# Last q and k of a batch kept on chip, v1, scores and the loads of x moved in a fused attention and triangle kernel

## The chip, the cores and the metric

One core of one Trainium2 chip. The metric is the device time of one execution in microseconds (us), lower is better. Most executions of a kernel agree within 0.3%. A ratio is the mean time of one kernel's runs over that of the kernel before in the same rounds on the same chip, so it is not quite the ratio of the medians that I quote. "Within 2%" counts as the same.

## The reference, cut to what matters

Input x has 4 batches of 64 x 64 tokens of 256 channels, all in float32. Layer 0 is self-attention over the 4096 tokens, layer 1 is a "triangle" attention followed by a layer norm, an MLP and a second layer norm.

```python
# layer 0
f, g, v = xt @ Wf + bf, xt @ Wg + bg, xt @ Wh + bh
beta = softmax(einsum('bqd,bkd->bqk', g, f))
x1 = x + (einsum('bqk,bkd->bqd', beta, v) @ Wo + bo)
# layer 1: 8 heads of 32
q, k, v1, v2 = (x1 @ W for W in (Wq, Wk, Wv1, Wv2))
scores = einsum('bilhd,bljhd->biljh', q, k) / sqrt(d_k)
att = softmax(scores, axis=2)
out = einsum('biljh,bilhd,bljhd->bijhd', att, v1, v2)
h = layer_norm(x1 + out @ Wo1)
out = layer_norm(relu(h @ W1 + b1) @ W2 + b2 + h)
```

## The kernel before

Each batch runs through three stages. In the **attention stage** TensorE computes layer 0, and between its products it projects the finished blocks of 512 tokens to q, k, v1 and v2, which go to DRAM. The **transition** finishes the last block, and computes the first scores of the triangle. The **triangle stage** has 4 pairs of heads with 8 steps each, 32 steps. In a step VectorE (DVE) and GpSimd (POOL) form eight products att x v2, TensorE sums them with v1 in its stationary tile ("wsel") into PSUM accumulators ("acc"), and ScalarE (ACT) copies these out. In every odd step the next pair's scores ("sp") are made as well. From batch 1 on, the MLP of the batch before fills holes of the step.

The profile lines leave numbers out of names. In them gf is g and f of one block of x, ahg and ahf are their places in DRAM, tp and yT are the turned block in PSUM and on chip, R and Rp are the products that DVE and POOL form, v1c is the loaded v1, S the scores after the exponential, es the weights, ao the copy of acc; nt, hT, mp, hid and zp belong to the MLP and its layer norms.

At the start, x of batch 0 comes block by block, each load issued just before it is turned. The tags name the buffer rings; "R" has three buffers, "qk" one:

```python
def turned(q):                                   # front0
    if q % 2 == 0:
        xt[q // 2] = work.tile([P, 8, C], F32, tag="R", name="xt", bufs=3)
    t = xt[q // 2][:, q % 2 * 4 : q % 2 * 4 + 4, :]
    nc.sync.dma_start(out=t, in_=xf[b, ts(q, 512), :]...)
    ...                                          # 8 transposes
for q in range(8):
    ahead = turned(q + 1) if q < 7 else None
    factors(...)                                 # g and f
    for w, n in enumerate(("g", "f")):
        nc.scalar.dma_start(out=d[n][q], in_=gf[:, w, 0:P])
    if ahead: taken(*ahead)                      # ScalarE and DVE copy the turned block
    ...                                          # v
    if q % 4 == 3: ...                           # spreads of g and f, sync queue
```

The end of the transition, where the last q and k pass through DRAM:

```python
proj(last, "q", 0, None, stage[0][:, 2, :])
proj(last, "k", 0, None, stage[0][:, 3, :])
L.fetch_qk(0, 1)                                 # the part just stored
...
more = [v1, q, k, v2 of the last block, second halves]
for u in range(4):
    L.scores(0, u); L.take_scores(); more[u]()
```

The start of a step:

```python
if step == 1: L.fetch_qk(1)
if scored: L.scores(pair + 1, ig // 2)
if waiting is not None:
    L.take(step - 1, 1, waiting); L.store(step - 1)
if step == 2: L.fetch_v2(1)
if ig == 0 and 0 < pair < NPAIR - 1: L.fetch_v2(pair + 1)
L.fetch_v1(step + 2)
if scored: L.take_scores() ...
if more and not late: L.stationary(step + 1)
L.product(step, Q_[0]); L.product(step, D_[0])
...
```

Of the kernel before, what the change touches and what calls it, by code (L numbers as in the profile page):

```python
# [33 lines left out]
def attention_then_triangle_kernel(  # L34
# [164 lines left out]



    def spread_g(F, r, d, q0=0, q1=8):
        nc.sync.dma_start(
            out=F.gT[ts(r, CQK), 512 * q0 : 512 * q1].rearrange("c (q t) -> c q t", t=P),
            in_=d[q0:q1].rearrange("q (n c) t -> c (q n) t", n=4),
        )

    def spread_f(F, q, d):
        nc.sync.dma_start(
            out=F.fT[ts(q % 4, CQK), q // 4, :].rearrange("c (n t) -> c n t", t=P),  # L210
            in_=d[q].rearrange("(n c) t -> c n t", n=4),
        )


    def front0(b):
        F = Front()
        for name in ("x0", "x1", "g", "f", "lo", "hi"):
            F.alloc(name)
        d = {n: dram.tile([8, P, P], F32, tag="ah" + n, name="ah" + n, bufs=NB) for n in ("g", "f")}
        xt = {}  # L220

        def turned(q):
            if q % 2 == 0:
                xt[q // 2] = work.tile([P, 8, C], F32, tag="R", name="xt", bufs=3)
            t = xt[q // 2][:, q % 2 * 4 : q % 2 * 4 + 4, :]
            nc.sync.dma_start(out=t, in_=xf[b, ts(q, 512), :].rearrange("(n p) c -> p n c", p=P))
            tp = pa("tp")
            for cc in range(2):
                for n in range(4):
                    nc.tensor.transpose(tp[:, cc, ts(n, P)], t[:, n, ts(cc, P)], ident)  # L230
            return q, tp

        def taken(q, tp):
            nc.scalar.copy(F.yT[0][:, ts(q, 512)], tp[:, 0, :])
            nc.vector.tensor_copy(F.yT[1][:, ts(q, 512)], tp[:, 1, :])

        taken(*turned(0))
        for q in range(8):
            ahead = turned(q + 1) if q < 7 else None
            col = ts(q, 512)  # L240
            gf = work.tile([P, 2, C], F32, tag="s4", name="gf")
            factors(pb("gf"), [F.yT[cc][:, col] for cc in range(2)], gf)
            for w, n in enumerate(("g", "f")):
                nc.scalar.dma_start(out=d[n][q], in_=gf[:, w, 0:P])
            if ahead:
                taken(*ahead)
            ps = pc("vp")
            for n in range(4):
                for cc in range(2):
                    nc.tensor.matmul(  # L250
                        ps[:, ts(n, P)], F.yT[cc][:, ts(q * 4 + n, P)], wh_sb[:, cc, :],
                        start=(cc == 0), stop=(cc == 1),
                    )
            nc.vector.tensor_copy(
                F.v[q // 4][:, q % 4 * 4 : q % 4 * 4 + 4, :], ps.rearrange("p (n d) -> p n d", n=4)
            )
            if q % 4 == 3:
                for r in range(4):
                    spread_f(F, q - 3 + r, d["f"])
                    spread_g(F, r, d["g"], q - 3, q + 1)  # L260
        return F


# [80 lines left out]
    def layer0(b, F, safe, rest):  # L344
# [152 lines left out]
        def proj1(qb, m, ps=None, st=None, queue=nc.sync):  # L497
# [11 lines left out]
                in_=st.rearrange("p (n c) -> p n c", n=2),  # L509
            )  # L510

        parts = [
            [norm, bounds],
            [output],
# [9 lines left out]
        for g in range(8 * NQB):  # L524
            qb, k = divmod(g, 8)
            if safe and k == 0 and qb + 1 < NQB:
                mx, todo = pieces(qb + 1)
                for qc, t in todo:
                    max_piece(qc, t, mx)
                row[qb + 1] = max_row(mx)  # L530
            if g + 1 < 8 * NQB:
                scores(g + 1)
            values(g)

            if qb > 0 and not (qb == last and k >= 6):
                for part in parts[k]:
                    part(qb - 1)
            if qb == last and k == 3:
                L.fetch_v1(0)
                L.fetch_v1(1)  # L540
            if qb == last and k == 5:
                if b > 0:
                    rest.load(NP * (b - 1))
                L.fetch_qk(0, 0)
        L.fetch_v2(0, 0)


# [14 lines left out]
        bounds(last)  # L562
        if old:
            rest.affine_a(t0)
            rest.turn(t0)
        proj(last, "q", 0, None, stage[0][:, 2, :])
        proj(last, "k", 0, None, stage[0][:, 3, :])
        L.fetch_qk(0, 1)
        if old:
            rest.load(t0 + 1)  # L570
            rest.residue(t0)
            mps = [rest.hidden(t0, fc, wide=True) for fc in range(4)]
            for fc in range(4):
                rest.rectify(t0, fc, mps[fc])
# [9 lines left out]
        for u in range(4):  # L584
            L.scores(0, u)
            L.take_scores()
            more[u]()
        L.sums(0)
        L.weights(0)
        L.turn(0)  # L590
# [7 lines left out]
    class Layer1:  # L598
# [6 lines left out]



        def fetch_qk(self, pair, part=None):
            io, rows = self.io, ts(pair, 64)
            if part != 1:  # L610
                self.qk[pair] = big.tile([P, 2, 2048], F32, tag="qk", name="qk")
            qk = self.qk[pair]
            i0, i1 = ((0, 56), (56, 64))[part] if part is not None else (0, 64)
            for lh in range(2):
                half = slice(64 * lh, 64 * lh + 64)
                nc.sync.dma_start(
                    out=qk[half, 0, 32 * i0 : 32 * i1],
                    in_=io["q"][rows, lh, i0:i1, :].rearrange("c i l -> c (i l)"),
                )
                a, e = max(i0 - 32 * lh, 0) * N, min(i1 - 32 * lh, 32) * N  # L620
                if a < e:
                    nc.sync.dma_start(
                        out=qk[half, 1, a:e], in_=io["k"][rows, 2048 * lh + a : 2048 * lh + e]
                    )


        def fetch_v2(self, pair, part=None):
# [336 lines left out]
    def run_layer1(b, L, rest, ahead, F):  # L964
# [7 lines left out]
        for step in range(NSTEP):  # L972
# [12 lines left out]
            k = L.npool(step)  # L985
            D_, Q_ = list(range(8 - k)), list(range(8 - k, 8))
            scored = step % 2 == 1 and pair + 1 < NPAIR
            if step == 1:
                L.fetch_qk(1)
            if scored:  # L990
                L.scores(pair + 1, ig // 2)
            if waiting is not None:
                L.take(step - 1, 1, waiting)
                L.store(step - 1)
# [1 line left out]
                L.fetch_v2(1)  # L996
            if ig == 0 and 0 < pair < NPAIR - 1:
                L.fetch_v2(pair + 1)
            L.fetch_v1(step + 2)
            if scored:  # L1000
                L.take_scores()
                if ig == 7 and pair + 2 < NPAIR:
                    L.fetch_qk(pair + 2)
            if more and not (scored and ig == NIG - 1):
                L.stationary(step + 1)

            late = scored and ig == NIG - 1

# [11 lines left out]
            L.accumulate(step, D_[0])  # L1020
            if behind is not None:
                ahead.values(behind)
            if more and late:
                L.stationary(step + 1)
            if not late:
                next_weights()
            if odd_a:
                rest.affine_a(nxt)
            if odd:
# [43 lines left out]
            if odd_a:  # L1073
                rest.rectify(nxt, 0, mps[0])
                rest.rectify(nxt, 1, mps[1])
            L.accumulate(step, Q_[1])
            if odd_a:
                mps = [rest.hidden(nxt, 2), rest.hidden(nxt, 3)]
                rest.rectify(nxt, 2, mps[0])
# [86 lines left out]
```

## Time and profile before

| | before |
|---|---|
| median of the first 3 runs | 4058.42 us (4054.1 to 4064.45) |
| profiled span, mean granted clock | 4059.6 us, 0.983 |
| TensorE (PE) busy | 93% |
| start, to the first scores of batch 0 | 54.65 us |
| first scores to the first attP copy, batch 0 | 458.95 us |
| steps of pairs 0 to 2, batch 0 | 361.3 us |
| the same, batches 1 to 3 together | 1181.7 us |

"attP copy" is ScalarE's copy of turned attention weights. It happens once a step, so 128 of these copies mark all steps; "pairs 0 to 2" runs from the first copy of a batch to the copy 25 steps later. From the page, the clock row (tenths in 40 slices of the span) and the last chain:

```profile
PEclk8999989999999999999999999999999998999999
...
PE 70%; DMA 7%; DVE 7%; ACT 6%; POOL 4%; issue 4%; SPq 2%; ACTq 0%; POOLq 0%; DVEq 0%
PE o L419 23%; PE acc L754 12%; PE proj L476 8%; PE s L397 7%; PE mp L893 5%; DVE R L745 4%; PE zp L908 4%; DMA v1c<-v1d 4%; POOL Rp L745 3%; PE v1p L501 3%; PE hp L800 2%; PE sp L650 2%; ACT es L687 2%; DMA qk<-k 1%; PE y L461 1%
```

The clock dips below 0.9 in the start, in the triangle stage of batch 0 and once late in batch 3. Loads of v1 (4%) and of q and k (1%) stand on the chain that ended last. The waits of batch 0's triangle stage (columns: total us, times, longest) name the same two:

```profile
ACT wsel L723 <- DMA v1c<-v1d: 13.7, 3, 6.5
...
PE sp L650 <- DMA qk<-k: 10.6, 2, 6.3
```

### The profile page before, as it was taken

How to read it: one execution, taken by the hardware profiler on the slowest of the kernel's cores; microseconds unless marked ns; L12 is line 12 of the kernel's file. 1: busy time of each engine (PE TensorE's matmuls, PEld its weight loads, DVE VectorE, ACT ScalarE, POOL GpSimd, SP SyncE). 2: the span in 40 equal slices, each digit the busy share in tenths (PEclk: the TensorE clock that was granted, in tenths of full speed). 3: DMA queues.
4: the chain of work that ended last, by engine and by line, in shares of the span. 5: the costliest groups of instructions: out<-in, count | busy, mean ns of one | idle time of the engine just before them, and what ended most of it. 6: DMA issues, size and time to landing. Idle time of an engine off the chain costs nothing.

```text
span 4059.6 us, 58989 instructions
## 1 busy us (share of the span) xinstructions
PE 3768.2 (93%) x23238; PEld 1761.1 (43%) x23238; DVE 2696.2 (66%) x2183; ACT 1812.7 (45%) x3737; POOL 1899.5 (47%) x976
## 2 busy tenths in 40 slices
PE   8999978889999989998999989999899998999988
PEld 4444433433444444443344444444344444444466
DVE  3444378897444379899544458899744437998955
ACT  2333355554333355554333345555433334555444
POOL 1000078895000079999000048899500007999944
PEclk8999989999999999999999999999999998999999
DMA  4111444543111433323111153232211143331122
GB/s 111 50 50 47 107 121 131 142 125 121 47 47 50 110 85 83 84 49 85 59 50 47 52 124 87 62 82 63 85 47 47 50 109 85 82 83 43 46 63 59
DMA packets 445199, 311.45 MB, mean 77 GB/s; under 512 B 298672, under 2 KB 410288, under 8 KB 437616
## 3 DMA queue, kind: packets, MB, share of 16 engines
q1 hardware_dynamic: 428320, 297.15, 27.6%
q10 hardware_dynamic: 15280, 7.54, 0.7%
q8 instruction: 185, 3.03, 0.3%
q0 software_dynamic: 1312, 2.89, 0.3%
q14 instruction: 102, 0.84, 0.1%
HBM read 166.93 MB, written 140.51 MB: 76 GB/s over the span
## 4 chain that ended last, share of the span: by engine, by line
PE 70%; DMA 7%; DVE 7%; ACT 6%; POOL 4%; issue 4%; SPq 2%; ACTq 0%; POOLq 0%; DVEq 0%
PE o L419 23%; PE acc L754 12%; PE proj L476 8%; PE s L397 7%; PE mp L893 5%; DVE R L745 4%; PE zp L908 4%; DMA v1c<-v1d 4%; POOL Rp L745 3%; PE v1p L501 3%; PE hp L800 2%; PE sp L650 2%; ACT es L687 2%; DMA qk<-k 1%; PE y L461 1%
## 5 line engine op out<-in xcount | busy, mean ns | idle before, releaser
L745 POOL TENSOR_TENSOR Rp<-attP,v 128x2048 f32<-128x2048 f32 x328 | 1490.4, 4569 | 713.0 <-ACT attP L704 586.6
L745 DVE TENSOR_TENSOR R<-att,v 128x2048 f32<-128x2048 f32 x696 | 1549.7, 2274 | 141.1 <-PE acc L754 90.1
L426 DVE TENSOR_TENSOR esum<-esum,e 128x2048 f32<-128x2048 f32 x224 | 512.8, 2289 | 592.3 <-ACT e L408 589.4
L754 PE MATMUL acc<-R,wsel 128*32 128x512 f32 x5568 | 730.3, 607 | 41.6 <-DVE R L745 38.3
L408 ACT ACTIVATE e<-s 128x1024 f32<-128x1024 f32 x512 | 496.6, 1021 | 408.3 <-PE s L397 380.6
L839 POOL TENSOR_SCALAR nt<-mv 128x4 f32<-128x4 f32 (+1 forms) x51 | 9.8, 193 | 1276.8 <-DVE mv L817 1272.7
L762 ACT COPY ao<-acc 128x1024 f32<-128x1024 f32 x256 | 259.2, 1012 | 597.6 <-PE acc L754 524.0
L419 PE MATMUL o<-e,vlo 128*128 128x512 f32 x1024 | 477.7, 610 | 0.0
L419 PE MATMUL o<-e,vhi 128*128 128x512 f32 x1024 | 472.7, 605 | 0.0
L754 PE MATMUL acc<-Rp,wsel 128*32 128x512 f32 x2624 | 340.9, 602 | 89.5 <-POOL Rp L745 44.0
L419 PEld LDWEIGHTS o<-e,vlo 128*128 128x128 f32 x1024 | 185.8, 191 | 283.7 <-issue 282.2
L397 PE MATMUL s<-gT,fT 32*128 32x512 f32 x2048 | 303.3, 641 | 4.8 <-ACT e L408 4.5
L419 PEld LDWEIGHTS o<-e,vhi 128*128 128x128 f32 x1024 | 184.7, 190 | 279.3 <-issue 279.3
L754 PEld LDWEIGHTS acc<-R,wsel 128*32 128x32 f32 x5568 | 143.8, 110 | 333.0 <-issue 200.9
L893 PE MATMUL mp<-hT,w 128*128 128x256 f32 x1024 | 253.2, 394 | 30.1 <-ACT hT L873 30.1
L687 ACT ACTIVATE es<-S,rd 128x64 f32<-128x64 f32 x1024 | 258.5, 335 | 8.7 <-DVE rd L679 7.1
L438 DVE RECIPROCAL rec<-den 128x512 f32<-128x512 f32 x32 | 107.4, 3358 | 215.6 <-PE den L436 215.6
L908 PE MATMUL zp<-w,hid 128*128 128x256 f32 x1024 | 246.1, 386 | 0.6 <-ACT hid L900 0.6
L893 PEld LDWEIGHTS mp<-hT,w 128*128 128x128 f32 x1024 | 185.8, 192 | 108.1 <-ACT hT L873 48.3
L908 PEld LDWEIGHTS zp<-w,hid 128*128 128x128 f32 x1024 | 187.1, 191 | 62.0 <-issue 40.2
L754 PEld LDWEIGHTS acc<-Rp,wsel 128*32 128x32 f32 x2624 | 70.2, 109 | 286.6 <-POOL Rp L745 108.1
L488 ACT COPY st<-proj 128x512 f32<-128x512 f32 x104 | 60.9, 585 | 293.7 <-issue 166.5
(140 smaller groups left out, 3791.9 us busy)
## 6 DMA issues: line engine op xcount, KB each, us to landing
v<-v2d SPq DMA_DIRECT2D x24, 1024.0 KB
v1c<-v1d SPq DMA_DIRECT2D x128, 128.0 KB
aT<-ao SPq DMA_DIRECT2D x1024, 16.0 KB
A<-aT SPq DMA_DIRECT2D x256, 64.0 KB
yc<-y SPq DMA_DIRECT2D x64, 256.0 KB
out_dram<-z SPq DMA_DIRECT2D x64, 256.0 KB
y<-yT SPq DMA_DIRECT2D x56, 256.0 KB
q<-st SPq DMA_DIRECT2D x56, 256.0 KB
```

Source lines behind the costliest of these rows:

```text
L397: nc.tensor.matmul(s_ps[r // 2][:, r % 2, :], fT[rows, tt, ts(n, P)], gT[rows, ts(qb, QB)], start=True, stop=not safe,)
L408: nc.scalar.activation(e[g][:, 2 * j : 2 * j + 2, :], s_ps[j], AF.Exp)
L419: nc.tensor.matmul(o_ps[qb], F.v[tt][:, r * 4 + n, :], es[:, r, :], start=(k == 0 and r == 0), stop=(k == 7 and r == 3),)
L426: nc.vector.tensor_tensor(esum[qb], esum[qb], es, ALU.add)
L476: nc.tensor.matmul(ps, w[:, cc, rows], y(qb, cc), start=(cc == 0), stop=(cc == 1))
L501: nc.tensor.matmul(ps[:, ts(n, C)], y(qb, cc)[:, ts(m * 2 + n, P)], wv1_sb[:, cc, :], start=(cc == 0), stop=(cc == 1),)
L687: nc.scalar.mul(self.e[:, i, :], rows[:, i, :], rec[:, i : i + 1])
L745: eng.tensor_tensor(R, src.unsqueeze(1).to_broadcast([P, D, N]), v2[:, h], ALU.mult)
L754: nc.tensor.matmul(acc[32 * c : 32 * c + 32, n % 2, :], w[:, n, c, 16 * h : 16 * h + 32], R[:, ts(c, 8), :].rearrange("p d j -> p (d j)"), ...
L762: nc.scalar.copy(self.ao[step][:, ts(np, 2)].rearrange("p k d j -> p k (d j)"), acc)
L893: nc.tensor.matmul(self.mp[:, fc % 2, :], w1_sb[:, cc, ts(fc, P)], self.hT[tt][:, cc, :], start=(cc == 0), stop=(cc == 1),)
L908: nc.tensor.matmul(self.zp[tt][:, n, :], self.hid[tt][:, fc, ts(n, P)], w2_sb[:, fc, :], start=(fc == 0), stop=(fc == 3),)
```

## The change

It has four parts: (1) all eight loads of x go first in the sync queue, the spreads of g and f move to GpSimd, and a block's g and f get a ring of three buffers of their own; (2) the last q and k of a batch are projected on two column halves so that ScalarE can copy them straight into the triangle's tile; (3) q and k of pair 1 are asked for at the end of the transition, and v1 at the start of a step, ahead of v2 and of the stores; (4) the scores move from the start of the odd step to the end of the even one, and the stationary tile is copied after the weights. The core of the diff:

```diff
+        for q in range(8):
+            nc.sync.dma_start(out=xt[q], in_=xf[b, ts(q, 512), :]...)
 ...
-                    spread_g(F, r, d["g"], q - 3, q + 1)
+                    spread_g(F, r, d["g"], q - 3, q + 1, nc.gpsimd)
 ...
+            two_halves(ps[0][:, 0:256], wq_sb, (one, one), halves)
+            two_halves(ps[1], wk_sb, (two, one), (ys, ys))
+            nc.scalar.mul(qk[:, 0, 1792:2048], ps[0][:, 0:256], scale1)
+            nc.scalar.copy(qk[64:128, 1, 1536:2048], ps[1][64:128, :])
 ...                                    (rows of pair 1: stage, three stores on ScalarE)
-        proj(last, "q", 0, None, stage[0][:, 2, :])
-        proj(last, "k", 0, None, stage[0][:, 3, :])
-        L.fetch_qk(0, 1)
+        proj_qk(L.qk[0], stage[0][:, 2:4, :])
 ...
             more[u]()
+        L.fetch_qk(1)
 ...
-            if step == 1:
-                L.fetch_qk(1)
+            L.fetch_v1(step + 2)
             if scored:
-                L.scores(pair + 1, ig // 2)
+                L.take_scores()
 ...
             L.accumulate(step, Q_[1])
+            if step % 2 == 0 and pair + 1 < NPAIR:
+                L.scores(pair + 1, ig // 2)
```

More of the change, by code (lines that the diff above doesn't have):

```diff
@@ L198, in factors, with spread_g @@
             nc.scalar.activation(t[:, w, 0:P], ps[:, w, :], AF.Identity, bias=bias)
-    def spread_g(F, r, d, q0=0, q1=8):
-        nc.sync.dma_start(
+    def spread_g(F, r, d, q0=0, q1=8, queue=nc.sync):
+        queue.dma_start(
             out=F.gT[ts(r, CQK), 512 * q0 : 512 * q1].rearrange("c (q t) -> c q t", t=P),
@@ L206, in spread_g, with spread_f @@
         )
-    def spread_f(F, q, d):
-        nc.sync.dma_start(
+    def spread_f(F, q, d, queue=nc.sync):
+        queue.dma_start(
             out=F.fT[ts(q % 4, CQK), q // 4, :].rearrange("c (n t) -> c n t", t=P),
@@ L219, in front0 @@
         d = {n: dram.tile([8, P, P], F32, tag="ah" + n, name="ah" + n, bufs=NB) for n in ("g", "f")}
-        xt = {}
-        def turned(q):
-            if q % 2 == 0:
-                xt[q // 2] = work.tile([P, 8, C], F32, tag="R", name="xt", bufs=3)
-            t = xt[q // 2][:, q % 2 * 4 : q % 2 * 4 + 4, :]
-            nc.sync.dma_start(out=t, in_=xf[b, ts(q, 512), :].rearrange("(n p) c -> p n c", p=P))
-            tp = pa("tp")
+        xt = [work.tile([P, 8, C], F32, tag="R", name="xt", bufs=3) for _ in range(3)]
+        xt.append(work.tile([P, 8, C], F32, tag="Rp", name="xt"))
+        xt = [xt[q // 2][:, q % 2 * 4 : q % 2 * 4 + 4, :] for q in range(8)]
+        for q in range(8):
+            nc.sync.dma_start(out=xt[q], in_=xf[b, ts(q, 512), :].rearrange("(n p) c -> p n c", p=P))
+        def turned(q):
+            t, tp = xt[q], pa("tp")
             for cc in range(2):
@@ L240, in front0 @@
             col = ts(q, 512)
-            gf = work.tile([P, 2, C], F32, tag="s4", name="gf")
+            gf = work.tile([P, 2, C], F32, tag="st", name="gf", bufs=3)
             factors(pb("gf"), [F.yT[cc][:, col] for cc in range(2)], gf)
@@ L258, in front0 @@
                 for r in range(4):
-                    spread_f(F, q - 3 + r, d["f"])
-                    spread_g(F, r, d["g"], q - 3, q + 1)
+                    spread_f(F, q - 3 + r, d["f"], nc.gpsimd)
+                    spread_g(F, r, d["g"], q - 3, q + 1, nc.gpsimd)
         return F
@@ L510, in proj1, with proj_qk, two_halves @@
             )
+        def proj_qk(qk, st):
+            ys = [y(last, cc) for cc in range(2)]
+            halves = [[t.rearrange("p (i o l) -> p o i l", o=2, l=32)[:, lh] for t in ys] for lh in range(2)]
+            ps = [pb("projq"), pb("projk"), pb("projq")]
+            def two_halves(ps, w, cols, moving):
+                for cc in range(2):
+                    for lh in range(2):
+                        nc.tensor.matmul(
+                            ps[ts(lh, 64), :], w[:, cc, cols[lh]], moving[lh][cc], start=(cc == 0), stop=(cc == 1)
+                        )
+            one, two = slice(0, 64), slice(64, 128)
+            two_halves(ps[0][:, 0:256], wq_sb, (one, one), halves)
+            two_halves(ps[1], wk_sb, (two, one), (ys, ys))
+            nc.scalar.mul(qk[:, 0, 1792:2048], ps[0][:, 0:256], scale1)
+            nc.scalar.copy(qk[64:128, 1, 1536:2048], ps[1][64:128, :])
+            two_halves(ps[2][:, 0:256], wq_sb, (two, two), halves)
+            nc.scalar.copy(st[0:64, 0, :], ps[1][0:64, :])
+            nc.scalar.dma_start(out=io["k"][64:128, ts(last, QB)], in_=st[0:64, 0, :])
+            nc.scalar.mul(st[:, 1, 0:256], ps[2][:, 0:256], scale1)
+            for lh in range(2):
+                nc.scalar.dma_start(
+                    out=io["q"][64:128, lh, ts(last, 8), :].rearrange("c i l -> c (i l)"),
+                    in_=st[ts(lh, 64), 1, 0:256],
+                )
         parts = [
@@ L543, in layer0 @@
                     rest.load(NP * (b - 1))
-                L.fetch_qk(0, 0)
+                L.fetch_qk(0, True)
         L.fetch_v2(0, 0)
@@ L564, in layer0 @@
             rest.affine_a(t0)
+        proj_qk(L.qk[0], stage[0][:, 2:4, :])
+        if old:
             rest.turn(t0)
-        proj(last, "q", 0, None, stage[0][:, 2, :])
-        proj(last, "k", 0, None, stage[0][:, 3, :])
-        L.fetch_qk(0, 1)
-        if old:
             rest.load(t0 + 1)
@@ L604, in __init__, with fetch_qk @@
             self.S, self.v2, self.qk, self.v1, self.att, self.ao = {}, {}, {}, {}, {}, {}
-        def fetch_qk(self, pair, part=None):
+        def fetch_qk(self, pair, first=False):
             io, rows = self.io, ts(pair, 64)
-            if part != 1:
-                self.qk[pair] = big.tile([P, 2, 2048], F32, tag="qk", name="qk")
-            qk = self.qk[pair]
-            i0, i1 = ((0, 56), (56, 64))[part] if part is not None else (0, 64)
+            qk = self.qk[pair] = big.tile([P, 2, 2048], F32, tag="qk", name="qk")
+            n = 56 if first else 64
             for lh in range(2):
-                half = slice(64 * lh, 64 * lh + 64)
+                half, lk = slice(64 * lh, 64 * lh + 64), min(n - 32 * lh, 32) * N
                 nc.sync.dma_start(
-                    out=qk[half, 0, 32 * i0 : 32 * i1],
-                    in_=io["q"][rows, lh, i0:i1, :].rearrange("c i l -> c (i l)"),
-                )
-                a, e = max(i0 - 32 * lh, 0) * N, min(i1 - 32 * lh, 32) * N
-                if a < e:
-                    nc.sync.dma_start(
-                        out=qk[half, 1, a:e], in_=io["k"][rows, 2048 * lh + a : 2048 * lh + e]
-                    )
+                    out=qk[half, 0, 0 : 32 * n], in_=io["q"][rows, lh, 0:n, :].rearrange("c i l -> c (i l)")
+                )
+                nc.sync.dma_start(out=qk[half, 1, 0:lk], in_=io["k"][rows, 2048 * lh : 2048 * lh + lk])
         def fetch_v2(self, pair, part=None):
@@ L998, in run_layer1 @@
                 L.fetch_v2(pair + 1)
-            L.fetch_v1(step + 2)
-            if scored:
-                L.take_scores()
-                if ig == 7 and pair + 2 < NPAIR:
-                    L.fetch_qk(pair + 2)
-            if more and not (scored and ig == NIG - 1):
-                L.stationary(step + 1)
+            if scored and ig == 7 and pair + 2 < NPAIR:
+                L.fetch_qk(pair + 2)
             late = scored and ig == NIG - 1
@@ L1022, in run_layer1 @@
                 ahead.values(behind)
-            if more and late:
-                L.stationary(step + 1)
             if not late:
                 next_weights()
+            if more:
+                L.stationary(step + 1)
             if odd_a:
```

## The prediction

> **What bounds the kernel now.** I read the page first, then a table by stage, then the waits and the timeline of every stage in which TensorE is not full. The page says that TensorE is the engine to watch:
>
> ```profile
> PE 3768.2 (93%) x23238; PEld 1761.1 (43%) x23238; DVE 2696.2 (66%) x2183; ACT 1812.7 (45%) x3737; POOL 1899.5 (47%) x976
> ```
>
> 93% is an average. By stage (columns: window, its length, then busy us of PE, weight load, DVE, ACT, POOL, then clock, DMA share, GB/s):
>
> ```profile
> 0.00:57.00 57.00, 37.40 (x462) 31.82 (x462) 10.47 (x17) 12.22 (x27) 18.32 (x37) 0.88 0.67 177
> 57.00:486.00 429.00, 428.04 (x1364) 179.25 (x1364) 204.88 (x128) 157.80 (x187) 0.00 (x0) 0.99 0.19 56
> 486.00:514.00 28.00, 18.53 (x280) 12.32 (x280) 0.94 (x3) 12.79 (x23) 0.00 (x1) 0.88 0.50 126
> 514.00:972.00 458.00, 387.19 (x4288) 177.24 (x4288) 396.24 (x230) 237.73 (x615) 399.17 (x88) 0.96 0.49 133
> 1430.00:1936.00 506.00, 455.46 (x3682) 211.10 (x3682) 455.90 (x378) 262.52 (x687) 463.83 (x254) 0.99 0.32 76
> ```
>
> The attention stage (57 to 486, and its three repeats of 413 us) has no gap: nothing is to be won there, and the change doesn't touch it. The triangle stage has 71 us of idle TensorE in batch 0 and about 50 in each later batch, while DVE, POOL and PE are each at 85 to 92%: no engine alone bounds it. So its time is balanced work plus waits, and the waits have names. The loads of x, at the start:
>
> ```profile
> 31.17 1.59 SPq L226 DMA_DIRECT2D xt<-in_x_dram  x3
> 36.98 1.94 PE L230 MATMUL tp<-ident,xt 128*128 128x128 f32 x8 [12.61 <-DMA xt<-in_x_dram]
> ```
>
> The last three loads stand in the sync queue behind the spreads of g and f. The last q and k of a batch, through DRAM and back:
>
> ```profile
> 492.72 0.44 PE L650 MATMUL sp<-qk 32*64 32x64 f32 x2 [6.85 <-DMA qk<-q]
> ```
>
> The q and k of pair 1, asked for only in step 1:
>
> ```profile
> 530.04 0.59 SPq L622 DMA_DIRECT2D qk<-k  x1
> 535.90 0.44 PE L650 MATMUL sp<-qk 32*64 32x64 f32 x2 [6.35 <-DMA qk<-k]
> 540.60 2.03 PE L650 MATMUL sp<-qk 32*64 32x64 f32 x62 [4.26 <-DMA qk<-k]
> ```
>
> And v1 of the next step, asked for right behind 2 MB of v2:
>
> ```profile
> 647.24 1.17 SPq L633 DMA_DIRECT2D v<-v2d  x2
> 648.46 0.59 SPq L712 DMA_DIRECT2D v1c<-v1d  x1
> 661.48 1.00 ACT L723 COPY wsel<-v1c 64x128 f32<-64x128 f32 x4 [6.45 <-DMA v1c<-v1d]
> 663.13 1.91 PE L699 MATMUL att<-ident,es 128*128 128x128 f32 x4 [5.38 <-ACT es L687]
> ```
>
> ScalarE works in order, so 128 KB of v1 that took 13 us stops the weights, the turn and TensorE. In a double step without such a wait (31.3 us in batches 1 to 3) little is lost:
>
> ```profile
> 3549.20 1.99 ACT L660 ACTIVATE S<-sp 128x512 f32<-128x512 f32 x2 [0.90 <-PE sp L650]
> 3551.29 1.07 PE L754 MATMUL acc<-Rp,wsel 128*32 128x512 f32 x8 [1.16 <-POOL nt L841]
> 3556.64 2.02 PE L893 MATMUL mp<-hT,w 128*128 128x256 f32 x8 [0.66 <-ACT hT L873]
> ```
>
> **The Trainium skill.** "DMA: Bandwidth & Descriptors", section "Queues, rings and completion order", says that descriptors of a ring are consumed in order; the v1 load that waits out v2's bytes agrees. Its section "Issuing engines are not separate DMA queues" says that another issuing engine saves only sequencer time: I give the spreads' move to GpSimd no bandwidth. "TensorE: Matmul & The Clock Gate", "Part 1: The HAM clock gate", says that an idle window of about 3.4 us halves the clock until as long a busy one; the trace agrees (eight transposes take 1.94 us after the 12.6 us gap, 1.04 elsewhere), so each long wait costs 1 to 4 us more than its idle time. "TensorEngine Tiling (Array Packing)", "Key Properties", says that column tiles run in parallel; in the trace four 32-column products of 512 take 1.0 us together, and one full 128-column product of 512 takes 0.94 (four records, two products, in 1.88).
>
> **The change, part by part.**
>
> *Loads of x.* All eight stand first in the sync queue. The 12.6 us gap and the half clock behind it could go, 13 to 14 us. But the built program shows on what each DMA waits: eight DMA semaphores serve the sync and ScalarE queues in turn, and a DMA waits until the last user of its semaphore has landed. In the changed program ScalarE's second store of f stands behind a small weight load that itself follows the seventh x load in the sync queue, and ScalarE's copies stand behind that store. By bytes, 3.5 MB of x beside some 2.4 of weights at the roughly 310 GB/s of 4 to 20 us is there at about 21 us; six more blocks at the present pace of 3.9 us and the tail put the first scores near 48 instead of 54.65. An estimate: 6 saved (2 to 11).
>
> *Last q and k.* Before: two projections, 4 products, 3.8 us on PE. After: 4 of 64x256, 4 of 64x512, 4 of 64x256, in pairs on two column halves: 0.94 + 1.88 + 0.94 = 3.8 us by the tiling above, so no more PE time. ScalarE gets four copies for two (about 0.7 us more) and three DMA issues of 0.4 to 0.6. In batch 0 the scores start right after the v1 projection (485.9) instead of 492.7, the short second wait goes, and the v1 projection behind it, 3.33 us at half clock, takes 1.89: 8 us. In batches 1 to 3 the first MLP fills that hole already (waits of 1.1 and 0.7 us): I give them 1 each, because the extra ScalarE work delays the turned h by about 3 us while the projection hides 1.65 of it. 3 together.
>
> *Fetch of pair 1 and of v1 earlier.* I measured steps from one attP copy to the same one 8 steps later, that is one pair. Batches 1 to 3: 131.0, 126.6, 126.7; 130.4, 130.8, 126.0; 135.5, 126.1, 126.1. Without waits a pair is three ordinary double steps of 31.3 and a last one of 30.4: 124.3. The excess is 11.3 + 14.3 + 14.8 = 40.4. In batch 0 pairs take 119.9, 116.2, 116.1, and undisturbed double steps 26.9, 25.8, 27.2, so 106.5 a pair: excess 32.7. The fetch of pair 1 moves some 20 us ahead of its first use, more than its 10.5 us of flight, and v1 is asked for before v2 and before the eight stores. Nearly all of the excess should go; I take 30 in batch 0 and 34 in the others, since some slow stretches there are half clock whose cause I can't name.
>
> *Scores at the end of the even step.* No work is removed. ScalarE copies the scores two products earlier and makes the weights before the stationary tile. In batch 0 the 2 us of scores fall where PE waits for POOL's third product. In batches 1 to 3 I walked through the double step: the product waited for at 3551.29 is bound by POOL and still starts at about 3551.5, since the first product of the odd step now waits for ScalarE to empty acc (see the rivals); the weights end about 1.5 us earlier, the turned h 0.4. Nine ordinary double steps in three batches, 0.35 each: 9 with rounding down. Batch 0: 3.
>
> Sum: 6 + 8 + 3 + 30 + 34 + 9 + 3 = 93. I give back 5 for waits that I don't see. 4058 - 88 = 3970.
>
> **Rivals.** (a) *A PSUM wait replaces the scores' place.* The accumulators and the scores share two buffers. Before, 2 us of scores stood between the last product into acc and the first that needs its buffer, and the copy (1.01 us) hid behind them. Now the scores go ahead, so that product waits 1.2 us. In batches 1 to 3 this falls into the 1.16 us wait for POOL; if it adds to it, 27 ordinary double steps lose 1 us each and the time is about 3997. (b) *Balanced engines hold the step anyway.* With DVE and POOL near 90%, freed PE time could end in waits for their products: POOL's chain through a double step is 29.9 of 31.3 us. That leaves the long stalls' gain whole, since all three engines stand in them, and takes the 9 + 3 away: 3982. (c) *DMA semaphores serialize the start and the three new stores on ScalarE:* the start gains nothing and each transition loses 2: about 3984. (d) *The whole gain:* start 13, no giving back, all 73 of excess, 0.7 an ordinary double step (27 of them, 19), the transitions: about 3940.
>
> **Range and chances.** The long stalls (qk, v1, batch 0's transition) are about 70 of the 88 and seen line by line, so slower is nearly excluded. What may fail is worth 10 to 25 up or down: 3945 to 3998. The 2% line is 4058.4 x 0.98 = 3977, 7 us from my middle: 0.62 faster, 0.37 within.
>
> **What would show it.** In the profile of the changed kernel: no wait of scores for qk over 1 us and none of the stationary copy for v1 over 1; batch 0's triangle stage some 33 us shorter, each later one 11 to 16; first scores near 48 us; PE waiting about 1.2 us for the copy of acc at the start of odd steps, and no longer for nt there. I am wrong if ordinary double steps come out above 31.5, if v1 is still late behind another transfer, or if the first scores come after 53.

## The result and the profile after

| | before | after |
|---|---|---|
| median | 4058.19 us (4 runs) | 3995.38 us (4 runs, 3994.48 to 3996.17) |
| ratio | | 0.9844, 95% interval 0.9827 to 0.9861 |
| profiled span, clock | 4059.6, 0.983 | 3992.6, 0.987 |

The kernel is 1.6% faster: within 2%, so "same", where I had given 0.62 to "faster". The time lies in my range (3945 to 3998), near its upper end. From the page of the changed kernel:

```profile
PE 3759.9 (94%) x23302; PEld 1751.7 (44%) x23302; DVE 2693.2 (67%) x2183; ACT 1812.8 (45%) x3745; POOL 1909.2 (48%) x992
...
PEclk9999999999999999999999999999999999999999
...
PE 72%; ACT 9%; DVE 5%; DMA 4%; SPq 3%; POOL 3%; issue 3%; ACTq 0%; DVEq 0%; POOLq 0%
```

The work is the same, the clock no longer dips below 0.9 in any slice, and DMA's share of the chain went from 7% to 4%. The table by stage (same columns as in the prediction; stage bounds moved with the kernel, and the attention stage is left out):

```profile
0.00:62.00 62.00, 40.24 (x460) 32.91 (x460) 10.56 (x17) 11.80 (x26) 25.39 (x49) 0.89 0.59 163
480.00:510.00 30.00, 26.50 (x320) 15.49 (x320) 4.08 (x7) 15.66 (x29) 0.00 (x0) 0.97 0.73 181
510.00:945.00 435.00, 385.01 (x4273) 176.59 (x4276) 396.20 (x230) 237.20 (x615) 399.36 (x88) 0.97 0.52 139
1406.00:1895.00 489.00, 452.45 (x3653) 209.28 (x3652) 451.76 (x377) 259.43 (x679) 460.24 (x252) 0.99 0.33 77
```

TensorE's idle time is 50 us in batch 0's triangle stage (71 before) and 37 in batch 1's (50). In the start it is 21.8 of 62 us, before 19.6 of 57: this stage got worse. By the attP copies, the 67.0 us between the two profiled spans (the medians differ by 62.8) divide as follows:

| part | predicted | measured |
|---|---|---|
| start (first scores 54.65 to 60.07) | -6 | +5.4 |
| batch 0, first scores to first attP copy | -8 | -9.2 |
| the same, batches 1 to 3 | -3 | -3.4 |
| batch 0, pairs 0 to 2 | -33 | -21.0 |
| batches 1 to 3, pairs 0 to 2 | -43 | -43.6 |
| last pairs of all batches, and the end | (+5 "unseen") | +4.8 |
| sum | -88 | -67.0 |

Two rows are off, by 11.4 and 12 us. First, the start: ScalarE's timeline there, with TensorE's line that waits for it and the two groups of the sync queue:

```profile
0.72 9.55 SPq L224 DMA_DIRECT2D xt<-in_x_dram  x8
10.32 35.76 SPq L137 DMA_DIRECT2D wo<-in_L_conv_Wo_dram  x32
```

```profile
22.21 0.33 ACTq L244 DMA_DIRECT2D ahg<-gf  x1
27.92 0.33 ACTq L244 DMA_DIRECT2D ahf<-gf  x1
28.29 0.58 ACT L234 COPY yT<-tp 128x512 f32<-128x512 f32 x1 [11.35 <-DMA ahg<-gf]
...
34.80 0.59 ACT L234 COPY yT<-tp 128x512 f32<-128x512 f32 x1 [2.95 <-DMA wo<-in_L_conv_Wo_dram]
```

```profile
28.93 1.38 PE L193 MATMUL gf<-yT,wg 128*32 128x128 f32 x16 [9.82 <-ACT yT L234]
```

No product waits long for x any more (the 12.6 us gap is gone). Instead ScalarE, in order, stands at the stores of g and f, and its copy of the next block behind them comes 11.35 us late. Later copies come 2.95, 2.48 and 3.76 us late, and for these three the trace names loads of wo1 (written "wo") as what ended the wait, although the stores need nothing of wo1. Before, those loads came after the start (from 57.86 us).

Second, batch 0. The first double step of pairs 1 and 2 takes 32.0 and 32.7 us, the others 25.8 to 26.8. Its timeline, cut to four lines:

```profile
634.49 1.17 SPq L654 DMA_DIRECT2D v<-v2d  x2
635.75 0.53 SPq L277 DMA_DIRECT2D xin<-in_x_dram  x1
...
648.71 1.94 PE L286 MATMUL tp<-ident,xin 128*128 128x128 f32 x8 [3.87 <-DMA xin<-in_x_dram]
650.58 1.66 PE L775 MATMUL acc<-R,wsel 128*32 128x512 f32 x8
```

"xin" is the next block of x for batch 1, turned in a hole of batch 0. It now stands where v1 stood before: behind 2 MB of v2. TensorE waits 3.87 us and then runs below full clock (1.94 us for eight transposes that take 1.09 elsewhere). The waits of the stage confirm both, and show one more at its start:

```profile
PE tp L286 <- DMA xin<-in_x_dram: 7.3, 2, 3.9
...
DVE R L766 <- DMA v2d<-stage: 4.8, 1, 4.8
```

DVE's third product waits for its buffer, which a store of v2 still reads. No wait of sp for q or k and no wait of wsel for v1 is in that list: parts (2) and (3) did what they were meant to.

In batches 1 to 3 all nine pairs 0 to 2 take 123.2 to 123.4 us (before 125.9 to 135.5). Four lines of TensorE from a double step of batch 3, with the scores in their new place (the view ends at 3553 us, which cuts the last group to three of its eight products):

```profile
3543.22 1.98 PE L671 MATMUL sp<-qk 32*64 32x64 f32 x64 [0.32 <-ACT ao L783]
3545.13 1.07 PE L775 MATMUL acc<-Rp,wsel 128*32 128x512 f32 x8
...
3547.43 1.07 PE L775 MATMUL acc<-R,wsel 128*32 128x512 f32 x8 [0.37 <-ACT S L681]
...
3552.40 0.94 PE L914 MATMUL mp<-hT,w 128*128 128x256 f32 x3 [0.66 <-ACT hT L894]
```

The wait that I expected for the PSUM buffer is there, but it is 0.3 to 0.4 us, not 1.2, and it ends with ScalarE's copy of the scores. The 1.16 us wait for POOL's nt is gone.

### The profile page after: what moved, and what is told of

Its sections match the earlier page's. It is cut to its first block, busy times and chain, and to the rows that moved or that the text cites. A ratio compares the mean times of both kernels' runs of the same rounds, so it can differ in the third digit from the quotient of the medians.

```text
span 3992.6 us, 59230 instructions
## 1 busy us (share of the span) xinstructions
PE 3759.9 (94%) x23302; PEld 1751.7 (44%) x23302; DVE 2693.2 (67%) x2183; ACT 1812.8 (45%) x3745; POOL 1909.2 (48%) x992
## 3 DMA queue, kind: packets, MB, share of 16 engines
q1 hardware_dynamic: 420320, 291.38, 27.7%
## 4 chain that ended last, share of the span: by engine, by line
PE 72%; ACT 9%; DVE 5%; DMA 4%; SPq 3%; POOL 3%; issue 3%; ACTq 0%; DVEq 0%; POOLq 0%
PE o L419 23%; PE acc L775 12%; PE proj L476 8%; PE s L397 7%; PE mp L914 5%; PE zp L929 4%; DVE R L766 3%; PE sp L671 3%; PE v1p L501 3%; ACT S L681 2%; POOL Rp L766 2%; ACT ao L783 2%; PE hp L821 2%; SPq L790 2%; PE y L461 1%
## 5 line engine op out<-in xcount | busy, mean ns | idle before, releaser
L681 ACT ACTIVATE S<-sp 128x512 f32<-128x512 f32 x128 | 130.7, 1129 | 83.9 <-PE sp L671 83.9
```

The lines of the kernel that those rows point to most:

```text
L681: nc.scalar.activation(self.S[pair][:, :, l0 : l0 + 8].rearrange("p i l -> p l i"), sp[:, lh], AF.Copy if self.safe else AF.Exp,)
```

## The experiments

Twelve runs followed, eleven variants and the changed kernel itself once more, which gives the spread. Each had at least five timings in rounds with the kernel before; all gave correct results. They fell on four chips, on which the kernel before had medians of 4058.8 to 4062.8 us, so compare ratios rather than medians between runs of different chips.

**The changed kernel again.**

> The changed kernel unchanged, beside the others on the same chip: 3992 to 4000, ratio to before 0.983 to 0.986; it gives the spread between chips and the base of the comparisons.

Measured: 3992.29 us, ratio 0.9842 (0.9829 to 0.9856), beside 0.9844. First scores 59.66. Its transition of batch 0 took 447.86 instead of 449.70 us, pair 0 of batch 0 122.0 instead of 118.8 with its first step, pairs 1 and 2 218.5 instead of 221.5. So a single stretch of batch 0 can differ by 3 us between two runs of one kernel; the three pairs together agree (340.35 and 340.55).

### The start

**The old start in the changed kernel.**

```diff
-        for q in range(8):
-            nc.sync.dma_start(out=xt[q], ...)
+        (inside turned: the load of block q, as in the kernel before)
-                    spread_f(F, q - 3 + r, d["f"], nc.gpsimd)
+                    spread_f(F, q - 3 + r, d["f"])     # spread_g and gf's buffers as well
```

> The changed kernel with the start of the kernel before (x loaded block by block, spreads on the sync queue, g and f of a block in the old buffers). In the traces the start is the only stage in which the change lost: first scores at 60.07 us, before at 54.65. If the start is separable, first scores come back to 54.6 +- 0.5, every later stage stays within 1 us of the changed kernel, and the time falls by 5.4 to about 3990. Rival: the later stages depend on how the start left the queues; then the gain is not 5.4 (under 3 or over 8).

Measured: 3988.89 us, ratio 0.9821. First scores 55.04, so the start itself is worth the 5 us. But the profiled span fell by 10.6, which is the rival's sign (over 8), and my claim that later stages stay within 1 us failed: the last pairs are 3.5 us shorter, two transitions 1.5 each, the end 1.3, batch 0 is 2.4 longer. The last step of batch 1's triangle stage shows what such a 1.5 is. Columns as in the table by stage; first the changed kernel, then this run:

```profile
1861.50:1880.00 18.50, 15.15 (x92) 6.72 (x95) 17.21 (x10) 7.99 (x23) 18.34 (x8) 0.91 0.27 80
```

```profile
1859.12:1876.12 17.00, 13.60 (x94) 6.51 (x95) 16.96 (x10) 8.00 (x23) 16.84 (x8) 1.00 0.29 87
```

In both, TensorE waits 2.7 us for a product of POOL. Behind this wait two products took 1.93 and 1.86 us in the one and 1.07 and 1.04 in the other: the granted clock is 0.91 in the one window and 1.00 in the other. The program of that stage is the same; what differs is its place in time. All changes of the granted clock in a trace lie on a grid of 3.41 us. Two of these windows of the changed kernel, the one with the wait and the one behind it:

```profile
1870.38:1873.79 3.41, 0.77 (x8) 0.00 (x0) 3.41 (x2) 3.40 (x12) 3.41 (x2) 1.00 1.01 303
1873.80:1877.21 3.41, 3.36 (x16) 0.59 (x16) 2.65 (x2) 0.38 (x2) 3.41 (x1) 0.50 0.36 106
```

In the first, TensorE is busy for 0.77 us only, and the second is at half clock. With the old start the same wait falls across two windows, with 1.58 and 2.50 us of matmuls, and the clock stays at 1.00. The two transitions are of the same kind: in batch 2, behind a wait of 2.01 us (1.39 us of matmuls in its window), the MLP's products mp take 5.43 us in the changed kernel and 3.75 in this run. So 1.5 us here and there comes and goes with the clock, and I don't count it for any part of the change. The 1.3 us of the end I did not trace.

**wo1 moved into the attention stage.**

```diff
-                load_wo1()
                 fold_bias()
 ...
             values(g)
+            if b == 0 and g == 16 and not safe:
+                load_wo1()
```

> The changed kernel with one thing moved: the 32 small loads of wo1 go out in the attention stage of batch 0 instead of right behind x. Theory S (DMA semaphores serialize): ScalarE's stores of g and f no longer stand behind a wo1 load, ScalarE's copies of x go on, first scores near 48 us (46 to 50), 12 us sooner than in the changed kernel, time about 3983. Rival B (the bytes: eight loads of x at once share what the queues move, so blocks land late whatever follows them): first scores stay at 59 to 61, time 3995.

Measured: 3982.49 us, ratio 0.9799. First scores 46.42 us, 13.6 sooner. Theory S stands, B falls: the same eight loads of x in the same order, and the start is faster than in either kernel. One wait was left:

```profile
28.72 0.33 ACTq L244 DMA_DIRECT2D ahf<-gf  x1
29.09 0.58 ACT L234 COPY yT<-tp 128x512 f32<-128x512 f32 x1 [5.76 <-DMA xt<-in_x_dram]
```

In the program as built, the order of semaphores says why: eight of them serve the DMAs of the sync and ScalarE queues in turn, and this store's was last used by the eighth load of x. The trace's own semaphore records agree: that load landed at 28.64 us, and the store went out at 28.72.

**The stores of g and f on GpSimd.**

```diff
-                nc.scalar.dma_start(out=d[n][q], in_=gf[:, w, 0:P])
+                nc.gpsimd.dma_start(out=d[n][q], in_=gf[:, w, 0:P])
```

> The changed kernel with the stores of g and f issued by GpSimd instead of ScalarE; wo1 stays right behind x. Theory S: what hurts is that ScalarE, in order, waits at a store; with the store elsewhere its copies go on, first scores 46 to 51, time 3983 to 3987. Rival B: nothing changes, 59 to 61 and 3995. A second rival, that the 32 wo1 loads themselves slow the transfers of x: the run with wo1 moved gains and this one does not.

Measured: 3985.63 us, ratio 0.9808, first scores 50.16. It gains 9.9 us with wo1 still in its place, so the wo1 loads are not what slows x: by the semaphore records the eighth load of x landed at 28.0 us here, 27.7 in the changed kernel and 28.6 with wo1 moved. What holds it now is another thing:

```profile
ACT gf L198 <- DMA ahf<-gf: 12.3, 1, 12.3
```

GpSimd's own loads of weights, many of them waiting for an earlier one, come before them, so it reaches the first of these stores only at 30 us; ScalarE waits 12.3 us for the buffer of gf. The number was as expected, but for a path that is half another one.

**wo1 moved, two loads of x behind stores.**

```diff
-        for q in range(8):
-            nc.sync.dma_start(out=xt[q], ...)
+        for q in range(6):
+            load(q)
 ...
                 nc.scalar.dma_start(out=d[n][q], in_=gf[:, w, 0:P])
+            if q < 2:
+                load(6 + q, nc.scalar)
```

> The changed kernel with wo1 moved as in the run before (first scores there 46.42), and the last two loads of x issued by ScalarE after its stores of blocks 0 and 1 instead of ahead of all stores. With wo1 moved one wait was left: ScalarE's store of f of block 3 stands from 23.1 to 28.7 us behind the last load of x, whose semaphore it needs. In the program built here that store's semaphore was last used by a store of block 1. Theory S: that wait goes with the half clock behind it, first scores at 40 to 43, time 4 to 6 under that of the run with wo1 moved. Rival B: the last blocks of x are only there at 28 to 30 us, PE waits for the bytes instead, first scores 45 to 47.

Measured: 3974.90 us, ratio 0.9795, first scores 41.47. The store that stood from 23.1 to 28.7 us goes out at once:

```profile
24.44 0.33 ACTq L248 DMA_DIRECT2D ahg<-gf  x1
24.81 0.75 ACTq L248 DMA_DIRECT2D ahf<-gf  x1
```

No product waits for x after the first block's 5.3 us. B falls again: the last load of x landed at 29.2 us, no sooner than before, and nothing waited for it. The ratio is only 0.0004 under that of the run with wo1 moved; that run had another chip and a slower kernel before (4062.80 against 4058.81), so I rely on the trace for the 5 us. Beside the changed kernel on the same chip it is 17.4 us faster.

### Batch 0's triangle stage

**The v2 store first.**

```diff
+            lambda: proj(last, "v2", 1, None, stage[1][:, 2, :], nc.scalar),
             lambda: proj1(last, 1, ...),
             lambda: proj(last, "q", 1, ...),
             lambda: proj(last, "k", 1, ...),
-            lambda: proj(last, "v2", 1, None, stage[2][:, 1, :], nc.scalar),
```

> The changed kernel with the last four projections of a batch in another order: v2 first, then v1, q, k (before: v1, q, k, v2), so that the slow scattered store of v2 goes out some 8 us earlier and no longer beside the early fetch of pair 1. Theory Q: the new wait at the start of a batch's triangle stage (DVE's third product waits for the store of v2 that still reads its buffer; 4.84 us in batch 0, 2 in the others) goes: first step of batches 1 to 3 from 9.5 to 9.8 back to 7.6 us, pair 0 of batch 0 from 109.4 to about 105, the stages about 10 shorter in all, first scores as in the changed kernel (60). Rival: whichever store is last waits behind the 2 MB of pair 1; then nothing moves and the wait names k.

Measured: 3990.29 us, ratio 0.9824. Batch 0 as theory Q says: pair 0 took 105.22 us, the three pairs together 3.8 less. Batches 1 to 3 as the rival says: batch 1's wait stayed (2.1 us) and named k. There the wait costs nothing, though: first step and pair 0 of batch 1 take 132.8 us in the changed kernel and 132.9 here; and where the first step took 7.6 instead of 9.6 (batch 3 here), the pair took 125.8 instead of 123.2. The next step takes the 2 us back.

**v2 of the next pair later.**

```diff
-            if step == 2:
-                L.fetch_v2(1)
-            if ig == 0 and 0 < pair < NPAIR - 1:
+            if ig == 3 and pair < NPAIR - 1:
                 L.fetch_v2(pair + 1)
```

> The changed kernel with the 2 MB fetch of the next pair's v2 three steps (one step in pair 0) later, in a step in which no block of x for the next batch is asked for. Theory X: in batch 0 that block of x stood behind v2 (PE waits 3.9 us for xin and then runs at half clock), so pairs 1 and 2 of batch 0 fall from 110.4 and 111.1 to 105 to 107, 9 us in all, and the wait for xin is gone; batches 1 to 3 stay at 123.2. Rival: v2 now stands before a v1 or behind the stores and another wait of the same size appears; pairs stay at 110 to 111.

Measured: 3984.30 us, ratio 0.9806. Pairs 1 and 2 of batch 0 took 106.0 and 104.5, and the wait for xin is gone; batches 1 to 3 stayed. Theory X stands. The two pairs are 11.0 us below the first trace of the changed kernel, but pair 0 came out 3 us longer, as in the repeated changed kernel; against that trace the two pairs gained 8.0 and the three together 8.3, so 8 is the safer figure.

### The parts alone

**Early v1 alone in the kernel before.**

```diff
             scored = step % 2 == 1 and pair + 1 < NPAIR
+            L.fetch_v1(step + 2)
 ...
-            L.fetch_v1(step + 2)
```

> The kernel before with one part of the change alone: v1 of the step after next is asked for at the start of a step, ahead of v2 and of the stores. Theory: the slow double steps of pairs 1 and 2 in batches 1 to 3 were v1 behind v2, so these six pairs fall from 126 to 131 to 124.5 (what they take with the scores in the old place); pairs 1 and 2 of batch 0 from 116 to about 111, where the wait for xin takes over; the pairs 0 keep most of theirs, for they wait for q and k of pair 1. Together 25 us, ratio to before 0.994. Rival: the order in the queue hides nothing because v2 is asked for one step too early anyway; pairs stay, ratio 1.000.

Measured: 4026.10 us, ratio 0.9914, more than expected (0.994). The six pairs fell to 124.5 us each, to the tenth; pairs 1 and 2 of batch 0 to 110.2 and 111.1, where xin takes over. In pair 0 of batch 1 the other wait is still there:

```profile
PE sp L650 <- DMA qk<-k: 4.4, 1, 4.4
```

**Early q and k of pair 1 alone in the kernel before.**

```diff
             more[u]()
+        L.fetch_qk(1)
 ...
-            if step == 1:
-                L.fetch_qk(1)
```

> The kernel before with another part of the change alone: q and k of pair 1 are asked for at the end of the transition, right after the last scores of pair 0, instead of in step 1. From attP(0) to the end of pair 0's steps the kernel before takes 129.0 us in batch 0 and 138.5, 138.0, 143.2 in batches 1 to 3; with early v1 alone 128.5 and 138.7, 138.4, 137.8; the changed kernel 118.8 and 132.8, 132.9, 133.2. Theory: what early v1 left there was the wait for q and k of pair 1, so here this stretch falls to about 120 in batch 0 and to 133 to 135 in batches 1 and 2, the later pairs stay as in the kernel before, about 20 in all, ratio to before 0.995. Rival: that gain is the scores' new place or needs both fetches; then under 8 in all, ratio over 0.998.

Measured: 4041.93 us, ratio 0.9949 as expected in sum, but not in its parts. Batch 0's stretch fell to 121.4. Batches 1 to 3 took 139.3, 135.8 and 140.2, where I had expected 133 to 135 in batches 1 and 2. With only one of the two loads early, the other still makes the stretch wait (4.4 us for k with early v1 alone, 1.6 to 2.4 for v1 here): early v1 alone takes 4.8 us from these three stretches together, early q and k alone 4.5, the changed kernel 20.8. Of the 20.8 the scores' place accounts for 3.3 (next run). The parts don't add. These waits account for part of the difference; the rest I did not trace, and both fetches without the change's other parts were not run.

**Scores back in the odd step.**

```diff
             if scored:
-                L.take_scores()
+                L.scores(pair + 1, ig // 2)
 ...                                   (take_scores and stationary behind the stores)
             L.accumulate(step, Q_[1])
-            if step % 2 == 0 and pair + 1 < NPAIR:
-                L.scores(pair + 1, ig // 2)
```

> The changed kernel with the scores and the stationary copy back in their old places in the odd step; the early fetches, the direct q and k and the start stay. If the scores' place is worth what I predicted (12), the time rises to about 4007 and ordinary double steps of batches 1 to 3 go from 31.0 to 31.3 or more. Rival (the wait for the copy of the accumulator takes it all back, so the place is worth nothing): 3995 +- 3, double steps stay at 31.0. In both cases there should be no wait for v1 over 1 us.

Measured: 4001.96 us, ratio 0.9850. Pairs of batches 1 to 3 took 124.3 to 124.7 instead of 123.2 to 123.4: 31.1 instead of 30.8 us for a double step on average, and 11.2 us for the nine pairs. Batch 0's three pairs took 339.2 instead of 340.4. The waits of late batch 3, 3300 to 3560 us; this run first, then the changed kernel:

```profile
PE acc L775 <- POOL nt L862: 8.2, 7, 1.2
```

```profile
PE acc L775 <- ACT S L681: 2.8, 8, 0.4
```

Seven waits of 1.2 us for POOL are replaced by eight of 0.4 us for ScalarE. The rival (the new wait takes it all back) falls in batches 1 to 3, and holds in batch 0, where nothing was gained. The whole-time ratio alone, 0.9850 against 0.9842, would not have told this.

**The last q and k through DRAM again.**

```diff
-        proj_qk(L.qk[0], stage[0][:, 2:4, :])
+        proj(last, "q", 0, None, stage[0][:, 2, :])
+        proj(last, "k", 0, None, stage[0][:, 3, :])
+        L.fetch_qk(0, 1)
```

> The changed kernel with the last q and k of a batch again through DRAM and back. If the direct write is worth what the traces say, batch 0 from first scores to the first attP copy goes from 449.7 (447.9 in two other runs) back to 457 to 459, batches 1 to 3 lose 1 us each, and the time rises by 11 against the changed kernel, ratio to before about 0.987. Rival: with the queues relieved by the other parts, the fetch lands in time anyway; 1 to 3 us only.

Measured: 4002.93 us, ratio 0.9852. The scores wait for q again, 6.59 us, but batch 0 from first scores to first attP copy took 454.7, not 457 to 459: the direct write is worth 5.0 us against 449.7, or 6.9 against the 447.9 that other runs of this code show. Batches 1 to 3 lost 3.7 together. The ratio came out at 0.9852 where 0.987 was expected. Some of the 9.2 us that the transition gained belongs to other parts; with early v1 alone it took 456.9.

### Together

The last run joins the four that helped: wo1 moved, x split, v2 store first, v2 later.

> The changed kernel with everything that helped alone: wo1 moved and x split (first scores 41), the v2 store first (pair 0 of batch 0 105 us), v2 of the next pair later (pairs 1 and 2 of batch 0 105 each). If they add, 19 + 4 + 11 = 34 less than the changed kernel, ratio to before 0.976, time about 3960. Rival: they share waits or contend, and the sum is under 25.

Measured: 3958.99 us (3956.68 to 3963.47), ratio 0.9755 (0.9741 to 0.9768): over 2% faster than the kernel before, and 33.3 us under the changed kernel on the same chip, where 34 was expected. First scores 41.76, batch 0's pairs 0 to 2 326.6 us. The profiled spans differ by less, 28.8 us: the start gives 17.9 and the three pairs 14.0, and batch 0's transition takes 3.4 back.

| run | median us | ratio to before | first scores | batch 0, pairs 0 to 2 | batches 1 to 3, pairs 0 to 2 |
|---|---|---|---|---|---|
| changed kernel | 3995.38 | 0.9844 | 60.07 | 340.4 | 1138.1 |
| changed kernel again | 3992.29 | 0.9842 | 59.66 | 340.6 | 1137.8 |
| old start | 3988.89 | 0.9821 | 55.04 | 341.1 | 1138.0 |
| wo1 moved | 3982.49 | 0.9799 | 46.42 | 343.3 | 1138.5 |
| g, f stores on GpSimd | 3985.63 | 0.9808 | 50.16 | 341.1 | 1139.3 |
| wo1 moved, x split | 3974.90 | 0.9795 | 41.47 | 340.3 | 1138.6 |
| v2 store first | 3990.29 | 0.9824 | 58.39 | 336.6 | 1138.5 |
| v2 later | 3984.30 | 0.9806 | 59.23 | 332.3 | 1138.2 |
| scores back | 4001.96 | 0.9850 | 60.21 | 339.2 | 1149.3 |
| q, k through DRAM | 4002.93 | 0.9852 | 59.27 | 343.1 | 1137.3 |
| all four | 3958.99 | 0.9755 | 41.76 | 326.6 | 1138.5 |
| before, early v1 | 4026.10 | 0.9914 | 55.35 | 349.9 | 1161.9 |
| before, early q and k | 4041.93 | 0.9949 | 54.64 | 350.7 | 1180.6 |

## Why the prediction was right or wrong

The middle was 3970, the time is 3995: 88 us expected, 62.8 found between the medians and 67.0 between the profiled spans. The range held; the chance of 0.62 for "faster" was on the wrong side, by the two steps that failed.

- **Loads of x: failed.** The step was "By bytes, 3.5 MB of x ... is there at about 21 us; six more blocks ... put the first scores near 48". I had read from the built program that ScalarE's store stands behind a small weight load, and then priced that wait by bytes and once. The bytes were right: by the trace's semaphore records the seventh load of x landed at 19.8 us. But the 8 KB load of wo1 behind it took until 27.84, and the store went out at 27.92; the store of g before it had stood until 22.2 for the semaphore of an earlier store. Together the first copy came 11.35 us late, and three more waits of 2.5 to 3.8 followed, because three later stores of f met other wo1 loads. This is my rival (c), which I gave a start that "gains nothing"; it lost 5.4. With the semaphores out of the way the start takes 41.5 to 46.4 us, so loading x first was right, and 13 us of gain (rival (d)'s figure) were there to have.
- **Batch 0's excess: mis-sized, by a wait not looked for.** The step was "Nearly all of the excess should go; I take 30". It assumed that v1 was the only load behind v2. The block of x for batch 1 was behind it as well, and had been hidden by the wait for v1: 8 to 11 us in two pairs, by which trace of the changed kernel one compares. The store of v2 that still held DVE's buffer took 3.8 more. Without both, pairs 0 to 2 of batch 0 take 326.6 us, about 35 less than before; I had said 33 with the scores' 3.
- **Batches 1 to 3: right, 43.6 against 43.** The excess gave less and the scores' place more: 11.2 by the run that takes it back, where I had 9. The rest, about 32, is the excess, for which I had 34. I hadn't said how much each of the two fetches depends on the other.
- **Scores' place, batch 0: wrong by its 3 us.** The run with the scores back shows no gain there. Why the 2 us of scores didn't fall into a hole I did not find; a difference of 1 to 2 us in batch 0 is also within what one kernel shows between two runs.
- **The PSUM wait (rival (a)): present, mis-sized.** 0.3 to 0.4 us, not 1.2. It ends with ScalarE's copy of the scores.
- **Last q and k: right.** 9.2 and 3.4 against 8 and 3, though 2 to 4 of the 9.2 come from other parts. The direct projection cost hardly more TensorE time, as the sum of 3.8 us said: 0.65, 0.65, 1.89 and 1.03 us of lines that overlap, from 482.6 to about 486.7, with a wait of 0.2 in it; the two projections before took 3.7. Rival (c)'s loss at the three stores didn't come.
- **The 5 us given back: right in size.** 4.8 us appear at the ends of stages; the part that I traced is clock that a shift in time takes or gives.

Of what I said would show it: no wait for q, k or v1, batch 0 33 shorter (21), the others 11 to 16 (14.5 on average), first scores near 48 (60), and "first scores after 53" is the sign that I had named for being wrong.

## What to carry to other kernels

When a load is moved first in a queue, look at who shares its completion semaphores and which engine waits in order at a DMA issue: a store that needs nothing from a load can stand behind it, and everything in that engine behind the store. When a long wait is removed, list every other transfer issued near it, not only the one that the profile named; the next one was hidden by the first. And measure parts both alone and taken out: two early loads gave 4.8 and 4.5 us alone and over 17 together with the rest of the change, since each alone leaves a wait for the other in the same stretch.

## What the Trainium skill lacked or had wrong

- "DMA: Bandwidth & Descriptors", section "Issuing engines are not separate DMA queues", says that issuing from several engines saves only sequencer time. For bandwidth nothing here contradicts it: the last load of x landed at 28.6 us issued by the sync queue and at 29.2 issued by ScalarE. It lacks that two issuing engines of a program can share completion semaphores (here eight for the sync and ScalarE queues), so that one stands at a store for the other's load; ScalarE's copies came 2.5 to 11.35 us late. Moving 32 small loads out of the way took the start from 60.07 to 46.42 us, and two loads of x issued by ScalarE, so that a store no longer had the semaphore of one still in flight, took it to 41.47.
- "TensorE: Matmul & The Clock Gate", section "Part 1: The HAM clock gate", gives an idle window of about 3.4 us, free-running, as what halves the clock. Here a wait of 2.7 us was followed by half clock in one run (1.93 us for what takes 1.07) and by full clock in another kernel whose program in that stage is the same (1.07). That it depends on the place in time agrees with "free-running". But the window needn't be idle throughout: windows of 3.41 us with 0.77 and 1.39 us of matmuls were followed by half clock, one with 1.58 was not. Counted over the traces of the kernel before and of the changed kernel, all 27 windows at full clock with under 1.4 us of matmuls were followed by one at half clock, and only four of some 2230 with over 1.85 us.
- No page that I read says how late GpSimd reaches a DMA issue that stands behind many loads of its own. With the stores of g and f moved there, it came to the first one only at 30 us, and ScalarE waited 12.3 us for a buffer.
